# Four more block products in quarter blocks, variances summed on ScalarE, one buffer for two products, in a four-layer graph kernel

## The chip, the cores and the metric

One core of a Trainium2 chip runs the whole kernel. Its engines are TensorE (PE, with PEld for its weight loads), VectorE (DVE), ScalarE (ACT), GpSimd (POOL) and SyncE (SP, which here only issues DMAs). Each engine executes its own instructions in the order in which they were put into its queue, and waits where an operand or a buffer isn't ready. The metric is the device time of one execution in microseconds, the median of several runs.

## The reference

128 graphs share one adjacency matrix of 128 nodes; each node has 512 features, all in float32. Four layers follow each other, each with a residual and a layernorm over the features.

```python
# x (128,128,512), adj (128,128)
def _L0(x):                       # GCN
    norm_adj = adj * rsqrt(deg)[:, None] * rsqrt(deg)[None, :]
    return einsum('nm,bmo->bno', norm_adj, einsum('bni,io->bno', x, weight)) + bias
def _L1(x):                       # W1 = W2 = adj
    A, C = adj @ x, adj @ x + b
    return max(relu(A[:, :, None, :] + (C - A)[:, :, :, None]), axis=-1)
def _L2(x):
    q, k, v = x @ Wq.T, x @ Wk.T, x @ Wv.T
    rel = adj.T[None] * einsum('bnd,bmd->bnm', q, k)
    rel = rel / norm(rel, axis=2, keepdims=True)
    return einsum('bnm,bmd->bnd', rel, v)
def _L3(x):                       # mask = adj, ALPHA = 0.2
    h = x @ W
    s1, s2 = h @ a[:512], h @ a[512:]
    e = leaky_relu(s1[:, :, None] + s2[:, None, :], ALPHA) * mask
    att = softmax(e, axis=2)
    return elu(att @ h + beta * h)
x = layernorm(x + L0(x)); x = layernorm(x + L1(x)); x = layernorm(x + L2(x)); x = layernorm(x + L3(x))
```

## The kernel before, in words

**Groups.** The 128 graphs are 32 groups of four (GB = 4). A group's `x` is one tile of 128 nodes x 4 graphs x 512 features that stays in SBUF from its load to its store. Layer 1 adds to a row a number that is the same for all its features (C - A is b), and the layernorm behind it takes that out again. So layers 0 and 1 together need one large product, layer 2 two, layer 3 one:

- `w`: `y` (x aggregated with the normalised adjacency, computed by the steps `y00` to `y11`) times the layer-0 weight. Its result is added to `x`; the two layernorms behind it are one, with other constants (`var`, case "w").
- `z`: the transposed `x` (`xT`) with the product of Wq and Wk (`gq`), laid down in C of z; `r` (line 905) multiplies it with `xT` to give q times k.
- `v`: `xT` with Wv, laid down in C of v; `f` (line 953) multiplies it with the normalised `rel`, and `fa` (line 963) adds it to `x`.
- `k`: `nT`, the transposed `x` after layer 2, with the layer-3 weight, laid down in C of k; `h` (line 953) multiplies it with the attention, and `em`, `ee`, `ea` form elu and the sum into `x`.

**Block products.** Each of the four products is done as seven products P1 to P7 of half size in place of eight (Strassen's scheme in Winograd's form), in the order 1, 2, 5, 7, 6, 3, 4. One block product is four matmuls of 128x256 (`make`, line 565). The left operands' sums are made by POOL (`sum`: steps `sy`, `sx`; tile `S`), the results are joined by ACT copies (`c`, `t`), DVE additions (`d`) and a POOL addition (`u`). The number behind a step's letter is the block product: `z6` is P6 of z, and P6, P3 and P4 add onto the banks of P1, P5 and P7.

**Quarter blocks.** A block product can itself be done by the same scheme on 128x128 blocks: seven matmuls of 128x128 (`make_small`, line 529; four first and three then, the three called with a second digit: `k28` is the second part of P2 of k). Before the three, ACT copies part of the bank away (`before`, steps `b..`, tile `q`) and DVE joins (`between`, steps `e..`, three operations, line 378). The left operand needs four sums of 128x128 on POOL (`small`, line 426, steps `ly`, `lx`, `ln`), the weight three sums more (`w_small`, made once). Before the change this is so for P2 of w, P1 and P2 of z and v, and P2 of k: six per group. The names are in `SMALL`; the sums of `xT` for P1 and P2 are kept in the tile `L`, because z and v both use them; those of P2 of y and n overwrite a part of the tile itself that isn't read any more (`room`).

**Turning.** `xT` and `nT` are made by DVE transposes of 32x32 squares (`xt`, `nt`, line 459) and 16 DMAs on SP's queue that exchange the squares (`xd`, `nd`, line 465). `rel` and the attention are turned likewise through DRAM (`wr`, `cr`, `aw`, `cat`). In the last group TensorE transposes `rel` and the attention.

**Layernorm.** `st` (bn_stats and bn_aggr on DVE, line 770), `va`, `po` (POOL), `nb`, then `ap` (ACT, line 796).

**Order.** Nothing is scheduled by a program at run time: three strings of steps, HEAD, TURN and TAIL, list every step as `group.step`, and each engine gets its instructions in that order. TURN is repeated with the group numbers raised by one: 21 turns, for groups 5 to 25 before the change. In one turn the work of four groups is interleaved: w of one group, z and v of the one before, k two before that, and the layernorm and store of a fourth. A tile of a pool is a slot that is used again by later groups; who writes to it first waits until the last reader of its earlier content is done. The pool `big` gives three slots to a name unless `bufs` says otherwise.

The lines that hold the order around P5 of z, before the change (group numbers relative):

```python
2.ea3 3.ex3 2.stk0 6.sy3 3.k7 3.ck5 2.stk1 6.bi01 2.stk2 3.k2 3.dk7 3.k6 3.bk2 2.stk3 3.ek2 3.k3
3.tk 3.uk11 2.vak 3.rd 3.k28 3.dk3 2.pok 3.k4 3.dk2 5.lx1 4.f0 2.nbk 4.f1 4.fa0 5.sx0 2.apk0
4.f2 3.dk4 2.apk1 2.fin0 5.lx2 4.fa1 4.f3 2.apk2 2.fin1 4.fa2 2.apk3
```

Of the kernel before, what the change touches and what calls it, by code (L numbers as in the profile page):

```python
# [41 lines left out]
EPS = 1e-5  # L43
# [3 lines left out]
GB = 4  # L47
# [3 lines left out]
FIRST = 5  # L51
LAST = -6
# [15 lines left out]
0.sq2 1.nbw s.mv1 0.sq3 1.apw0 0.v2 2.sy3 0.cv5 1.xt0 0.cr 1.apw1 0.v7 0.dv2 0.rp 1.apw2 1.xt1
2.bi10 1.apw3 1.xt2 0.v6 0.dv7 2.bi00 1.xt3 0.v3 0.tv 1.xd s.mv2 0.uv11 0.v4 0.dv3 2.bi11 0.f0
0.dv4 2.bi01 0.f1 0.fa0 0.f2 0.stv0 0.f3 0.fa1 0.fa2 3.y10 0.fa3 3.y00 3.cy10 3.bi10 0.stv1  # L70
3.y11 3.cy00 0.stv2 3.bi00 3.y01 3.cy11 0.stv3 3.sy0 2.w1 3.cy01 0.vav 0.pov 2.w5 2.dw1 3.sy1
2.w7 0.nbv 2.dw5 1.lx1 0.apv0 0.apv1 0.nt0 2.w2 0.apv2 2.dw7 1.sx0 0.nt1 2.w6 0.apv3 0.nt2 1.lx2
2.bw2 2.ew2 2.w3 2.tw 0.nt3 1.sx1 0.sc00 2.w28 1.sx2 2.dw3 2.w4 0.sc01 3.ly2 0.sc10 1.z1 0.nd
0.sc11 1.z5 1.bz1 1.sx3 0.sc20 1.ez1 3.sy2 1.z2 0.sc21 1.z18 1.bz2 2.uw01 0.sc30 1.z7 1.cz1
1.ez2 1.cz5 3.sy3 1.z6 0.sc31 2.uw10 1.dz7 2.dw2 2.uw11 1.z28 2.dw4 1.z3 3.bi11 1.dz2 1.tz
2.stw0 1.z4 1.uz11 0.pw 1.dz3 2.stw1 3.bi01 1.r0 1.dz4 2.stw2 1.r1 0.sn0 2.stw3 1.r2 0.pe 0.sn1
2.vaw 1.r3 1.v1 1.rm 2.pow 1.sq0 1.v5 0.sn2 1.bv1 0.pl0 1.ev1 0.pl1 0.sn3 0.pl2 1.v2 0.pl3 1.sq1
1.rt 1.v18 0.ej 1.bv2 1.v7 1.wr 1.cv1 1.ev2 1.sq2 1.cv5 2.nbw 0.ei 1.v6 2.apw0 1.dv7 2.apw1
2.xt0 1.cr 2.apw2 1.v28 2.xt1 1.v3 1.tv 1.dv2 2.apw3 1.uv11 2.xt2 0.ex0 2.xt3 1.v4 0.ex1 1.dv3
0.ex2 0.ex3 3.w1 2.xd 1.dv4 1.sq3 0.rd 1.rp 3.w5 3.dw1 0.so0 0.so1 3.w7 3.dw5 0.at 3.w2 3.dw7  # L80
3.w6 3.bw2 3.ew2 3.w3 3.tw 3.uw01 3.w28 3.uw10 3.dw3 0.aw 3.w4 3.dw2 3.uw11 3.stw0 1.f0 3.dw4
1.f1 3.stw1 2.lx1 0.cat 1.f2 3.stw2 1.f3 3.stw3 2.sx0 0.k1 1.fa0 2.lx2 3.vaw 1.fa1 0.k5 1.fa2
0.ck1 1.fa3 2.sx1 1.stv0 0.k7 0.ck5 2.sx2 1.stv1 1.stv2 3.pow 0.k2 0.dk7 2.sx3 0.k6 0.dk2 3.nbw
1.stv3 3.apw0 0.k3 s.m32 0.tk 3.apw1 3.xt0 0.uk11 3.apw2 0.k4 0.dk3 3.apw3 3.xt1 3.xt2 4.y10
0.dk4 4.y00 4.cy10 4.bi10 3.xt3 4.y11 4.cy00 1.vav 3.xd 4.bi00 4.y01 4.cy11 4.sy0 0.h0 4.cy01
0.h1 0.em0 4.sy1 0.h2 0.ee0 0.em1 0.ea0 4.sy2 0.h3 0.ee1 0.em2 2.z1 4.ly2 0.em3 0.ee2 2.z5 0.ea1
2.bz1 0.ee3 2.ez1 4.sy3 2.z2 0.ea2 1.pov 2.z18 2.bz2 0.ea3 2.z7 2.cz1 2.ez2 4.bi11 2.cz5 0.stk0
4.bi01 2.z6 2.dz7 0.stk1 2.z28 2.tz 3.sx0 0.stk2 2.z3 2.dz2 2.uz11 0.stk3 2.z4 2.dz3 3.sx1 0.vak
2.r0 1.nbv 2.dz4 0.pok 1.apv0 2.r1 1.apv1 1.nt0 3.sx2 2.r2 1.apv2 0.nbk 2.r3 1.apv3 1.nt1 3.sx3
1.nt2 0.apk0 2.v1 2.rm 0.apk1 0.fin0 2.v5 1.nt3 2.bv1 0.fin1 0.apk2 2.ev1 2.v2 0.apk3 0.fin2  # L90
2.rt 2.sq0 2.v18 0.fin3 1.sc00 2.bv2 2.v7 2.wr 2.cv1 2.ev2 2.sq1 2.cv5 1.sc01 2.v6 2.sq2 2.sq3
5.ld 2.dv7 2.rp 2.cr 1.sc10 2.v28 2.tv 1.sc11 2.v3 3.lx1 2.dv2 1.sc20 2.v4 2.uv11 2.dv3 1.sc21
3.lx2 3.z1 1.sc30 1.nd 2.dv4 3.z5 3.bz1 3.ez1 3.z2 1.sc31 3.z18 3.bz2 3.ez2 3.z7 3.cz1 3.cz5
3.z6 3.dz7 3.z28 3.tz 3.z3 3.dz2 3.uz11 3.z4 1.pw 3.dz3 3.r0 3.dz4 3.r1 1.sn0 3.r2 1.pe 1.sn1
3.r3 2.f0 3.rm 1.sn2 2.f1 3.sq0 2.fa0 3.sq1 1.ln2 2.f2 2.stv0 1.pl0 1.pl1 2.f3 2.fa1 1.pl2 1.pl3
1.sn3 2.fa2 4.w1 3.sq2 3.sq3 2.fa3 1.ej 2.stv1 4.w5 4.dw1 3.rp 2.stv2 4.w7 4.dw5 2.stv3 4.w2
4.dw7 2.vav 4.w6 4.bw2 1.ei 2.pov 4.ew2 1.ex0 1.ex1 4.w3 3.rt 1.ex2 1.ex3 2.nbv 3.wr 2.apv0 1.rd
4.w28 4.dw3 1.so0 2.apv1 4.w4 2.nt0 2.apv2 1.so1 4.dw2 2.apv3 2.nt1 3.v1 3.cr 2.nt2 4.tw 3.v5
3.bv1 2.nt3 4.uw01 3.ev1 4.uw10 2.nd 3.v2 1.at 3.v18 3.bv2 4.uw11 4.stw0 3.v7 3.cv1 3.ev2 3.cv5
4.dw4 3.v6 3.dv7 4.stw1 3.v28 3.tv 4.stw2 3.v3 3.uv11 4.stw3 3.dv2 3.v4 3.dv3 4.vaw 2.sc00 4.pow  # L100
5.y10 3.dv4 1.aw 5.y00 5.cy10 5.bi10 5.y11 5.cy00 4.nbw 2.sc01 5.bi00 4.apw0 5.y01 2.sc10 4.apw1
1.k1 2.sn0 1.cat 4.xt0 4.apw2 2.sc11 4.apw3 2.sn1 1.k5 4.xt1 1.ck1 4.xt2 5.cy11 2.sn2 4.xt3
5.cy01 1.k7 1.ck5 2.ln2 2.sc20 2.sc21 1.k2 1.dk7 2.sn3 1.k6 1.bk2 2.sc30 1.ek2 5.sy0 1.k3 1.tk
2.sc31 5.sy1 2.pw 1.k28 1.dk3 1.uk11 1.k4 1.dk2 5.ly2 3.f0 4.xd 1.dk4 5.sy2 3.f1 3.fa0 3.f2
3.stv0 5.bi11 3.f3 3.fa1 3.fa2 5.sy3 1.h0 3.fa3 1.h1 5.bi01 1.em0 1.h2 1.em1 1.ee0 1.h3 1.em2
1.ee1 2.k1 1.ea0 1.ee2 1.em3 1.ea1 1.ee3 2.k5 1.ea2 2.ck1 1.ea3 2.pe 2.k7 1.stk0 2.ck5 1.stk1
1.stk2 2.k2 2.dk7 4.lx1 2.k6 2.bk2 2.pl0 2.ek2 2.pl1 2.pl2 2.k3 2.pl3 4.sx0 1.stk3 2.tk 3.stv1
4.lx2 2.k28 1.vak 3.stv2 2.k4 3.stv3 4.sx1 2.dk3 4.z1 3.vav 4.sx2 2.dk2 4.z5 4.bz1 2.dk4 1.pok
4.ez1 4.z2 4.sx3 4.z18 4.bz2 1.nbk 4.ez2 2.ej 4.z7 1.apk0 4.cz1 1.fin0 3.pov 2.ei 1.apk1 4.z6
1.apk2 2.uk11 1.fin1 1.apk3 1.fin2 4.z28 3.nbv 4.cz5 1.fin3 4.dz2 4.tz 4.z3 4.dz7 2.ex0 2.ex1  # L110
4.uz11 2.ex2 4.z4 4.dz3 2.ex3 6.ld 3.apv0 2.rd 2.so0 4.r0 4.dz4 3.apv1 3.nt0 4.r1 3.apv2 2.so1
3.nt1 3.apv3 4.r2 3.nt2 4.r3 3.nt3 5.w1 2.at 3.nd 4.rm 3.sc00 4.sq0 5.w5 4.sq1 5.dw1 4.sq2
3.sc01 4.sq3 5.w7 4.rp 5.dw5 3.sc10 3.sc11 5.w2 5.dw7 5.w6 5.bw2 3.sc20 5.ew2 5.w3 5.tw 3.sc21
5.uw01 3.sc30 5.w28 5.uw10 5.dw3 2.aw 5.w4 5.dw2 5.uw11 3.sc31 4.v1 5.dw4 3.pw 4.v5 4.bv1 5.stw0
3.sn0 2.cat 4.ev1 3.sn1 4.v2 5.stw1 4.v18 4.bv2 3.sn2 5.stw2 3.pe 4.v7 4.cv1 4.ev2 3.ln2 4.cv5
# [12 lines left out]
2.aw 3.vav 3.pov 4.z4 4.dz3 3.nbv 3.apv0 2.cat 4.r0 4.dz4 3.apv1 3.nt0 4.r1 3.apv2 3.sc00 3.apv3
# [1031 lines left out]
```

## Time and profile before

| | us |
|---|---|
| median of 3 runs (lowest, highest) | 2022.32 (2022.27, 2022.95) |
| the profiled execution | 2021.49 |
| its span | 2019.7 |
| PE busy, share of the span | 1992.9, 99% |
| DVE busy | 1645.2, 81% |
| POOL busy | 1330.2, 66% |
| ACT busy | 829.7, 41% |
| one turn | 61.38 |

The span lasts from the first to the last instruction of the profiled execution; its time has 1.8 us more around it. Busy time is the sum over an engine's instructions, so overlaps with other engines aren't seen in it. The profile's matmul rows count each float32 matmul as two (it makes two passes). In a row such as `x<-p_w,x` the tile written stands left of the arrow, those read right of it, with buffer numbers left out. A release `<-DVE e L972` names the engine and the line whose result ended a wait.

Three of the costliest groups of instructions, from the list of the page (columns: line, engine, operation, tiles, shape, count, busy us, mean ns of one, idle time before them and its releaser):

```profile
L796 ACT ACTIVATE x<-x,nb,r 128x512 f32<-128x512 f32 x383 | 282.5, 804 | 188.9 <-DVE nb L790 176.9
L381 POOL TENSOR_TENSOR x<-x,bias_bc 128x512 f32<-128x512 f32 x128 | 162.7, 1291 | 37.1 <-PE py L736 28.9
L770 DVE BATCH_NORM_STATS2 st_v<-x 128x6 f32<-128x512 f32 x128 | 87.2, 681 | 0.2
```

### The profile page before, as it was taken

Reading aid. Unit: us, or ns where it says so; the run is one execution under the profiler, and the core shown is the slowest. Engines: PE = TensorE matmul, PEld = TensorE weight load, DVE = VectorE, ACT = ScalarE, POOL = GpSimd, SP = SyncE. Lnnn points to the kernel's source line nnn. Section 1 sums busy time; section 2 is a strip of 40 time slices with the busy share of each in tenths; the row PEclk is TensorE's granted clock in tenths of the full one; section 3 lists DMA queues with packets and bytes.
Section 4 is the critical chain, followed back from the end, with each engine's and each line's share of the span. In section 5 each row is a group of like instructions: output and inputs, shape, how many; then the busy total and the mean of one; then the engine's idle time right before and its main releaser. Section 6 shows DMA issues by size and latency. Waiting matters only on the chain.

```text
span 2019.7 us, 32758 instructions
## 1 busy us (share of the span) xinstructions
PE 1992.9 (99%) x10921; PEld 1715.3 (85%) x10921; DVE 1645.2 (81%) x3490; ACT 829.7 (41%) x1797; POOL 1330.2 (66%) x1429
## 2 busy tenths in 40 slices
PE   9899999999999999999999999999999999999997
PEld 8798888888888888888888888888888888888875
DVE  6878788888888888888888888888888888888886
ACT  2234334444344443444443444433444434444344
POOL 7677557766668666677666677666676668567551
PEclk9999999999999999999999999999999999999998
DMA  7433344443444444434344444444344444443443
GB/s 225 82 66 80 68 87 103 90 78 90 102 90 96 83 83 97 95 91 97 69 95 105 89 94 83 81 94 103 89 97 75 87 101 88 96 102 65 70 85 88
DMA packets 737975, 184.78 MB, mean 91 GB/s; under 512 B 689936, under 2 KB 690320, under 8 KB 737808
## 3 DMA queue, kind: packets, MB, share of 16 engines
q1 hardware_dynamic: 737664, 182.56, 41.8%
q8 instruction: 88, 1.44, 0.3%
q14 instruction: 79, 0.65, 0.1%
q10 hardware_dynamic: 144, 0.13, 0.0%
HBM read 64.55 MB, written 49.87 MB: 57 GB/s over the span
## 4 chain that ended last, share of the span: by engine, by line
PE 97%; SPq 1%; DVE 1%; DMA 0%; issue 0%; ACT 0%; POOL 0%; DVEq 0%; POOLq 0%
PE p_k L565 16%; PE p_w L565 16%; PE p_z L565 14%; PE p_v L565 13%; PE pr L905 6%; PE py L736 6%; PE pl_v L953 5%; PE pl_k L953 5%; PE p_z L529 5%; PE p_v L529 5%; PE p_k L529 2%; PE p_w L529 2%; SPq L465 1%; PE pk L827 1%; DVE e L972 0%
## 5 line engine op out<-in xcount | busy, mean ns | idle before, releaser
L796 ACT ACTIVATE x<-x,nb,r 128x512 f32<-128x512 f32 x383 | 282.5, 804 | 188.9 <-DVE nb L790 176.9
L381 POOL TENSOR_TENSOR x<-x,t_w 128x512 f32<-128x512 f32 x96 | 120.8, 1285 | 122.1 <-ACT t_w L375 122.1
L381 POOL TENSOR_TENSOR x<-x,bias_bc 128x512 f32<-128x512 f32 x128 | 162.7, 1291 | 37.1 <-PE py L736 28.9
L378 DVE TENSOR_TENSOR x<-p_w,x 128x512 f32<-128x512 f32 x192 | 129.4, 687 | 57.6 <-PE p_w L565 38.6
L972 DVE SCALAR_TENSOR_TENSOR e<-x,wa_bc 128x512 f32<-128x512 f32 x256 | 173.2, 676 | 3.8 <-ACT x L796 0.9
L384 POOL TENSOR_TENSOR r<-n,minus_half 128x4 f32<-128x4 f32 x32 | 32.4, 1012 | 174.5 <-ACT pr L920 174.5
L384 POOL TENSOR_TENSOR r<-v,minus_half 128x4 f32<-128x4 f32 (+1 forms) x99 | 98.9, 999 | 52.8 <-DVE v L782 44.4
L736 PEld LDWEIGHTS py<-nadjT,x 128*128 128x128 f32 x1024 | 120.3, 193 | 2.8 <-DVE nadjT L633 0.8
L963 DVE SCALAR_TENSOR_TENSOR x<-pl_v,r,x 128x512 f32<-128x512 f32 x128 | 90.1, 743 | 39.5 <-PE pl_v L953 38.7
L565 PE MATMUL p_z<-S_x,gq 128*128 128x256 f32 x512 | 121.2, 380 | 0.0
L565 PE MATMUL p_v<-wvT,S_x 128*128 128x256 f32 x512 | 121.1, 379 | 0.0
L565 PE MATMUL p_z<-S_x,gq_t 128*128 128x256 f32 x512 | 121.1, 379 | 0.0
L736 PE MATMUL py<-nadjT,x 128*128 128x128 f32 x1024 | 120.6, 277 | 0.4 <-DVE nadjT L633 0.4
L565 PE MATMUL p_v<-wvT_t,S_x 128*128 128x256 f32 x512 | 121.0, 379 | 0.0
L565 PE MATMUL p_w<-w_t,S_y 128*128 128x256 f32 x512 | 121.0, 379 | 0.0
L565 PE MATMUL p_w<-w,S_y 128*128 128x256 f32 x512 | 120.9, 379 | 0.0
L565 PE MATMUL p_k<-w_t,S_n 128*128 128x256 f32 x496 | 118.4, 382 | 0.0
L565 PE MATMUL p_k<-w,S_n 128*128 128x256 f32 x496 | 117.2, 379 | 0.0
L953 PE MATMUL pl_v<-C_v,relT 128*128 128x512 f32 x248 | 111.6, 592 | 0.0
L953 PE MATMUL pl_k<-C_k,attT 128*128 128x512 f32 x248 | 111.5, 592 | 0.0
L1061 DVE SCALAR_TENSOR_TENSOR x<-pl_k,x 128x512 f32<-128x512 f32 x127 | 86.8, 688 | 29.7 <-PE pl_k L953 29.4
L565 PEld LDWEIGHTS p_w<-w,S_y 128*128 128x128 f32 x512 | 97.3, 190 | 13.2
(1580 smaller groups left out, 5425.2 us busy)
## 6 DMA issues: line engine op xcount, KB each, us to landing
out_dram<-x SPq DMA_DIRECT2D x127, 256.0 KB, 2.0
x<-in_x_dram SPq DMA_DIRECT2D x31, 1024.0 KB, 5.3
d_r<-ru SPq DMA_DIRECT2D x31, 256.0 KB, 2.3
relT<-d_r SPq DMA_DIRECT2D x124, 64.0 KB, 2.5
s<-d_s SPq DMA_DIRECT2D x31, 256.0 KB, 3.7
d_a<-au SPq DMA_DIRECT2D x31, 256.0 KB, 2.0
attT<-d_a SPq DMA_DIRECT2D x124, 64.0 KB, 2.5
x<-in_x_dram SPq DMA_DIRECT2D x2, 512.0 KB, 4.4
```

The lines of the kernel that those rows point to most:

```text
L378: nc.vector.tensor_tensor(o, a, b, f)
L381: nc.gpsimd.tensor_tensor(o, a, b, f)
L384: nc.gpsimd.tensor_tensor(o, v, minus_half[:, : v.shape[-1]], ALU.pow)
L529: nc.tensor.matmul(self.banks[i][:, r, bass.ts(c, P)], lhsT=lhsT, rhs=rhs, start=(not then and n == 0), stop=(n == len(steps) - 1), skip_g ...
L565: nc.tensor.matmul(ps[:, j, :], lhsT=lhsT, rhs=rhs, start=(i not in ONTO and j == 0 and kc == 0), stop=(j == 1 and kc == 1), skip_group_ch ...
L736: nc.tensor.matmul(o, lhsT=self.x_chunk(b, kc), rhs=nadjT, start=True, stop=True)
L796: nc.scalar.activation(xt, xt, AF.Identity, bias=self.nb[k][:, b : b + 1], scale=self.rstd[k][:, b : b + 1],)
L905: nc.tensor.matmul(self.pr[:, b, :], lhsT=self.whole["z"][:, fc, b // 2, bass.ts(b % 2, P)], rhs=self.xT.chunk(b, fc), start=(fc == 0), st ...
L953: nc.tensor.matmul(ps, lhsT=left[:, b, :], rhs=self.whole[k][:, b, :], start=True, stop=True)
L963: nc.vector.scalar_tensor_tensor(xt, self.pf[b], self.rnorm[:, b : b + 1], xt, ALU.mult, ALU.add)
L972: nc.vector.scalar_tensor_tensor(wide(self.e), self.x[:, b, :], 1.0, wide(wa_bc[k]), ALU.mult, ALU.mult, accum_out=self.s[:, k, b : b + 1],)
L1061: nc.vector.scalar_tensor_tensor(xt, self.pz[b], 0.0, xt, ALU.max, ALU.add)
```

## The change

- **Quarter blocks.** P1 of w, P5 of z and v, and P1 of k are done by quarter blocks too: ten per group in place of six. POOL makes 12 more sums of 128x128 per group (`ly1`, `ln1`, `lx5`). Those for P1 of y and of n go into a new tile `l` with one slot, shared by the two; `L` has room for three sets. The second part of a small product is split into two steps (`18` and `19`: the first of the three matmuls, and the other two).
- **Variances of the layernorms of layers 2 and 3.** `fa` and `ea` write the rows' sums as they add (`accum_out`), DVE scales them (`mn`), ACT squares the centred `x` with the sum of squares as a by-product (`vq`, eight per turn; the squares themselves go into relT or attT and aren't read), and `var` and `shift` take these sums. bn_stats and bn_aggr fall away there, except for the last group.
- **Buffers.** C of z and C of v share one slot; rel and relT share a name; Setup's tiles move to other slots.
- **Attention.** The scaling by 1/den (`so0` to `so3`) is done by ACT, one graph at a time, in place of one POOL operation.
- **Ends.** x of group 0 and n of the last group are transposed by TensorE and copied by ACT (`xp`, `xc`, `np`, `nc`) in place of the exchange; s2 of the last group comes from four matmuls of 128x512.
- **Weight sums** for quarter blocks are made by POOL.
- **Order.** HEAD, TURN and TAIL are written anew; TURN runs for groups 6 to 26 (21 turns).

The part of the new TURN around P1 of k and the end of a turn, with the steps that end the turn:

```python
2.h2 2.ee0 2.em1 6.bi00 2.h3 2.em2 2.ee1 3.k1 6.ly2 2.em3 2.ee2 3.k7 2.ea0 3.bk1 2.ee3 3.ek1
6.ly1 3.k5 2.ea1 2.ea2 6.sy2 3.k18 3.k19 2.ea3 3.k2 3.ck1 6.bi11 2.mnk0 3.pw 2.mnk1 2.mnk2
2.vqk0 2.mnk3 3.k6 6.sy3 3.ck5 3.bk2 3.dk7 3.k3 2.vqk1 6.bi01 3.ek2 2.vqk2 5.lx1 3.pe 3.k28
3.k29 2.vqk3 3.k4 3.dk2 3.tk 2.vak 5.sx0 3.dk3 4.f0 3.dk4 5.sx1 3.pl0 4.f1 4.fa0 3.pl1 3.pl2
5.lx5 4.f2 4.fa1 3.pl3 4.f3 4.fa2
```

The first steps of TURN, which follow there with all numbers one lower for the same group (`4.z1` is z of the group that was 5):

```python
4.z1 3.mnv0 4.lx2 3.fa3 3.vqv0 4.z5 3.mnv1 3.mnv2 4.bz1 3.mnv3 3.vqv1 4.z7 4.ez1 4.sx2 3.vqv2
```

And around P1 of w:

```python
3.nt1 6.ld 5.w5 2.ex0 5.dw7 2.ex1 3.nt2 2.ex2 3.nt3 5.w1 2.ex3 5.dw5 3.nd 5.w4 5.bw1 2.rd 2.so0
5.ew1 2.so1 2.so2 2.so3 5.w18 5.dw4 2.so4 5.w19 5.w2 5.dw1 2.at 5.w3 5.bw2 5.ew2 5.w6 5.dw3
```

The diff without the three strings, cut to what the text speaks of:

```diff
-    def w_small(w, m, i):
-        b = lambda k, j: w[:, 2 * (i - 1) + k, bass.ts(j, P)]
+    def w_small(w, t, m, i):
+        of = w_blocks(w, t)[i]
+        b = lambda k, j: of[:, k, bass.ts(j, P)]
         return dict(
...
     W = {k: w_blocks(*v) for k, v in weights.items()}
-    SMALL = ("02", "g1", "g2", "v1", "v2", "32")
+    SMALL = ("01", "02", "g1", "g2", "g5", "v1", "v2", "v5", "31", "32")
     w_m = {k: wts.tile([P, 3, P], F32, name=f"m_{k}") for k in SMALL}
-    W2 = {k: w_small(weights[k[0]][0], m, int(k[1])) for k, m in w_m.items()}
+    W2 = {k: w_small(*weights[k[0]], m, int(k[1])) for k, m in w_m.items()}
...
         def small(self, i):
-            a = lambda b, k: self.chunk(b, 2 * (i - 1) + k)
+            of = self.s[:, 0] if i == 5 else self.block(0, i - 1)
+            a = lambda b, k: of[:, k, b, :]
             s = self.room(i)
...
         def room(self, i):
-            return [self.chunk(2 + n // 2, n % 2) for n in range(4)]
+            if i == 2:
+                return [self.chunk(2 + n // 2, n % 2) for n in range(4)]
+            t = big.tile([P, 4, P], F32, tag="l", name=f"l_{self.name}", bufs=1)
+            return [t[:, n] for n in range(4)]
...
+        def turn(self, b, x):
+            ps = bank(f"pt_{self.name}_{b}")
+            for kc in range(KC):
+                nc.tensor.transpose(ps[:, kc, :], x[:, bass.ts(kc, P)], ident)
+            self.banks[b] = ps
+        def take(self, b, sums):
+            if b == 0:
+                self.aT = big.tile([P, KC, GB, P], F32, tag="aT", name=f"{self.name}T")
+                if sums:
+                    self.s = big.tile([P, 4, 2, 2, P], F32, tag="S", name=f"S_{self.name}")
+            copy(self.aT[:, :, b, :], self.banks[b])
         def move(self):
...
             if i == 1:
-                self.l = big.tile([P, 2, 4, P], F32, tag="L", name=f"L_{self.name}", bufs=1)
-            return [self.l[:, i - 1, n] for n in range(4)]
+                self.l = big.tile([P, 3, 4, P], F32, tag="L", name=f"L_{self.name}", bufs=1)
+            return [self.l[:, {1: 0, 2: 1, 5: 2}[i], n] for n in range(4)]
...
-        def make_small(self, i, then=False):
-            if not then:
+        def make_small(self, i, then):
+            if then is None:
                 self.banks[i] = psum.tile([P, 2, HD], F32, tag="bank", name=f"p{i}_{self.name}")
             A, B = self.left.smalls[i], W2[f"{self.weight}{i}"]
-            steps = self.THEN_SMALL if then else self.FIRST_SMALL
+            steps = {None: self.FIRST_SMALL, 8: self.THEN_SMALL[:1], 9: self.THEN_SMALL[1:]}[then]
             for n, (r, c, a, b) in enumerate(steps):
...
             if i in self.left.smalls:
-                self.make_small(i, then is not None)
+                self.make_small(i, then)
                 return
...
         def xd(self):
-            self.xT.move()
+            if self.g:
+                self.xT.move()
+        def xp(self, b):
+            self.xT.turn(b, self.x[:, b, :])
+        def xc(self, b):
+            self.xT.take(b, True)
...
         def nd(self):
-            self.nT.move()
+            if not self.end:
+                self.nT.move()
+        def np(self, b):
+            self.nT.turn(b, self.x[:, b, :])
+        def nc(self, b):
+            self.nT.take(b, False)
...
+        def mean(self, k, b):
+            of = self.nm[k][:, b : b + 1]
+            nc.vector.tensor_scalar(of, of, -1.0 / D, None, ALU.mult)
+        def square_sum(self, k, b, junk):
+            if b == 0:
+                self.ss[k] = self.small("ss")
+            nc.scalar.activation(
+                wide(junk),
+                self.x[:, b, :],
+                AF.Square,
+                bias=self.nm[k][:, b : b + 1],
+                accum_out=self.ss[k][:, b : b + 1],
+            )
+        def row_sums(self, k, b):
+            if self.end:
+                return {}
+            if b == 0:
+                self.nm[k] = self.small("nm")
+            return dict(accum_out=self.nm[k][:, b : b + 1])
         def var(self, k, b=None):
...
             b = slice(0, GB) if b is None else slice(b, b + 1)
+            if k in self.ss:
+                nc.vector.tensor_scalar(self.var_[k], self.ss[k], 1.0 / D, EPS, ALU.mult, ALU.add)
+                return
             v, var = self.var_[k][:, b], self.mv[k][:, b, 1]
...
             b = slice(0, GB) if b is None else slice(b, b + 1)
+            if k in self.ss:
+                tt(self.nb[k], self.nm[k], self.rstd[k], ALU.mult)
+                return
             nc.vector.scalar_tensor_tensor(
...
                 shape = [P, KC, 2, 2 * P] if k == "z" else [P, GB, D]
-                self.whole[k] = big.tile(shape, F32, tag=f"{k}C", name=f"C_{k}_{self.g}", bufs=1)
+                tag = "kC" if k == "k" else "C"
+                self.whole[k] = big.tile(shape, F32, tag=tag, name=f"C_{k}_{self.g}", bufs=1)
                 self.po[k].block = lambda p, h: self.c_block(k, p, h)
...
         def rm(self):
-            self.rel = mid.tile([P, GB, P], F32, tag="rel", name=f"rel_{self.g}")
+            self.rel = mid.tile([P, GB, P], F32, tag="relT", name=f"rel_{self.g}")
             tt(self.rel, self.pr, adjT_b, ALU.mult)
...
             nc.vector.scalar_tensor_tensor(
-                xt, self.pf[b], self.rnorm[:, b : b + 1], xt, ALU.mult, ALU.add
+                xt, self.pf[b], self.rnorm[:, b : b + 1], xt, ALU.mult, ALU.add, **self.row_sums("v", b)
             )
...
             if self.end:
-                s2 = lambda b: self.s[:, 1, b : b + 1].to_broadcast([P, P])
-                self.s2 = self.transpose("ps2", s2).rearrange("p b j -> p j b")
+                ps = bank("ps2")
+                for kc in range(KC):
+                    wa2 = setup.wa_[:, 1, kc : kc + 1].to_broadcast([P, P])
+                    nc.tensor.matmul(
+                        wide(ps),
+                        lhsT=wa2,
+                        rhs=wide(self.nT.aT[:, kc]),
+                        start=(kc == 0),
+                        stop=(kc == KC - 1),
+                    )
+                self.s2 = ps.rearrange("p b j -> p j b")
                 return
...
                 nc.vector.scalar_tensor_tensor(e, e, rden, beta_i, ALU.mult, ALU.add)
-            elif i == 0:
-                pool_tt(self.e, self.e, self.rden.unsqueeze(2).to_broadcast([P, GB, P]), ALU.mult)
+            elif i < GB:
+                e = self.e[:, i, :]
+                nc.scalar.activation(e, e, AF.Identity, scale=self.rden[:, i : i + 1])
             else:
...
             xt = self.x[:, b, :]
-            nc.vector.scalar_tensor_tensor(xt, self.pz[b], 1.0, xt, ALU.min, ALU.add)
+            nc.vector.scalar_tensor_tensor(
+                xt, self.pz[b], 1.0, xt, ALU.min, ALU.add, **self.row_sums("k", b)
+            )
```

## The prediction

> **What bounds the kernel now.** I read the page's busy shares first, then the chain that ended last, then the windows of single turns and of the two places with holes, then TensorE's waits.
>
> ```profile
> PE 1992.9 (99%) x10921; PEld 1715.3 (85%) x10921; DVE 1645.2 (81%) x3490; ACT 829.7 (41%) x1797; POOL 1330.2 (66%) x1429
> ...
> PE 97%; SPq 1%; DVE 1%; DMA 0%; issue 0%; ACT 0%; POOL 0%; DVEq 0%; POOLq 0%
> ```
>
> ```profile
> 54.60:62.71 8.11, 0.02 (x1) 0.03 (x1) 7.99 (x16) 0.59 (x1) 2.87 (x3) 0.79 0.65 92
> 952.12:1013.50 61.38, 61.38 (x341) 53.01 (x340) 50.77 (x108) 25.99 (x56) 41.62 (x46) 1.00 0.43 91
> 1013.50:1074.88 61.38, 61.38 (x341) 53.01 (x340) 50.09 (x108) 25.83 (x56) 41.59 (x46) 1.00 0.43 91
> 1966.66:1970.54 3.88, 0.00 (x0) 0.03 (x1) 3.81 (x9) 1.12 (x2) 0.50 (x1) 1.00 0.66 100
> 1970.00:1975.10 5.10, 1.51 (x5) 0.77 (x5) 4.89 (x15) 0.00 (x0) 0.00 (x0) 0.57 0.67 102
> 1975.10:1978.60 3.50, 3.50 (x10) 2.75 (x10) 3.40 (x9) 1.14 (x4) 1.27 (x1) 0.50 0.46 114
> ```
>
> ```profile
> PE p_z L565 <- DMA x_0T<-sq_x: 8.1, 1, 8.1
> PE ps L896 <- DVE e L972: 6.9, 4, 3.9
> ```
>
> The columns of the windows are PE, PEld, DVE, ACT and POOL busy, then the granted clock. A turn is 61.38 us of matmuls in 61.38 us: nothing waits in the middle, so a matmul saved there is time saved, as long as nothing else becomes late. TensorE's holes are at the two ends.
>
> **1. Quarter blocks.** A whole block product starts 1.73 us after the one before it (1004.22, 1005.95, 1007.67); a quarter-block product takes 0.89 us (1003.33 to 1004.22) plus 0.67 (1007.67 to 1008.34), 1.56 in all:
>
> ```profile
> 1003.33 0.38 PE L529 MATMUL p_k<-w,n_14T 128*128 128x128 f32 x2
> 1003.55 0.61 PE L529 MATMUL p_k<-m,n_14T 128*128 128x128 f32 x4
> 1004.00 0.39 PE L529 MATMUL p_k<-w,n_14T 128*128 128x128 f32 x2
> 1004.22 1.89 PE L565 MATMUL p_k<-w_t,S_n 128*128 128x256 f32 x8
> 1005.95 1.89 PE L565 MATMUL p_k<-w,S_n 128*128 128x256 f32 x8
> 1007.67 0.61 PE L529 MATMUL p_k<-w,n_14T 128*128 128x128 f32 x4
> ```
>
> The built program has 492 fewer 128x256 and 861 more 128x128 matmuls: 123 products (z5, v5, w1 31 each, k1 30). 123 x 0.165 = **-20.3 us**; a full turn falls to 61.38 - 4 x 0.165 = 60.72.
>
> **2. Other engines, per turn.** ACT gains eight Squares of 128x512. The trace has none; the 128x512 Identity (0.80) and the 128x128 Square plus its accumulator read (0.28 + 0.19) bound one at 0.71 to 0.99, so 8 x 0.85 = 6.8. With four copies of 0.37 and four scalings of about 0.35, ACT goes from 26 to 36. DVE loses 8 x (0.68 + 0.18) of statistics and gains 4 x 1.23 of joining, 8 accumulator reads of 0.08 and 8 one-column scalings of 0.15: 50.4 - 6.9 + 6.8 = 50.3. POOL gains 12 sums of 0.45 and loses one 1.04: 46. All lie below 60.7, so by load TensorE still binds; the shared buffer C costs nothing, since the last reader of C of v (f) is issued before z's first copy and the last of z (r) before v's. The 32 exchange issues fewer on SP only bring loads forward. The square's unused result goes to relT or attT, read for the last time by f or h just before, and rel takes a slot of relT: 0, by the same order. The ten weight sets' sums go to POOL (40 x 0.45 = 18 us; DVE had 24 such sums); TensorE has other groups' products there: 0, at most +2.
>
> **3. Start.** x_0's exchange becomes 16 transposes (four take 0.43, so 1.72). The hole of 8.09 goes, and with it the slow clock after it: z of group 0 took 14.00 us, where seven block products at full clock take 12.09. Group 0's products run earlier, before other groups' x can fill (x_0 lands at 12.0): a new 1.55 of idle. -8.09 - 1.91 + 1.72 + 1.55 = -6.7. Group 1 and 3 then run nearer to their sums and joins (z5, pr): some 0.2 to 0.7 each, +1.7 (0 to 3). **-5.0**.
>
> **4. The small buffer "l", the step that decides.** Quarter sums of y and of n share one buffer. In the built program POOL's first sum for ly1 of group g+2 waits for the first matmul of k19 of g-1, the last reader of n's sums; it is written ahead of k5 in the order, so without that wait POOL could take it 2 us earlier or more (k5 1.73 and k18 0.22). Behind it on POOL stand, in order, sy2, bi11, sy3, bi01, lx1, sx0, sx1 and lx5 of g+1, and z5's second matmul of that next group needs lx5's third sum. The durations:
>
> ```profile
> 1057.35 2.50 POOL L381 TENSOR_TENSOR S_y<-y_18T 128x512 f32<-128x512 f32 x2
> 1059.81 1.28 POOL L381 TENSOR_TENSOR S_y<-S_y,y_18T 128x512 f32<-128x512 f32 x1
> 1061.04 1.83 POOL L381 TENSOR_TENSOR y_18T<-y_18T 128x128 f32<-128x128 f32 x4
> 1062.83 1.28 POOL L381 TENSOR_TENSOR S_y<-y_18T,S_y 128x512 f32<-128x512 f32 x1
> ```
>
> Pitch 1.23 for 128x512, 1.79 for four of 128x128. POOL: 1.79 + 4 x 1.23 + 1.79 + 2 x 1.23 + 1.29 = 12.25, plus some 0.3 to hand over (a matmul's end 0.165, then 0.08 as from py at 1053.58 to bias at 1053.66, and again). TensorE's work from k19 to that matmul: 0.22 + k2 0.89 + k6, k3 3.45 + k28, k29 0.67 + k4 1.73 + f 3.43 + z1 0.89 + 0.22 = 11.50. Late by 1.05; 0.75 if the handovers cost nothing, 1.45 at the sums' mean durations of 1.29. It comes once for each of groups 6 to 27: 22 x 1.0 = **+22** (16 to 32). A second small wait: between w1's first four matmuls and w19 TensorE has w4 and one matmul, 1.95; the end 0.165, ACT's copy 0.37, the three joins 1.23 and three handovers of 0.08 make 2.0 to 2.15. About 0.15 x 29 groups = **+4** (0 to 6).
>
> VectorE's small operations can stand still beside a POOL sum:
>
> ```profile
> 497.46 1.20 DVE L790 SCALAR_TENSOR_TENSOR nb<-mv_w,r 128x4 f32<-128x4 f32 x1
> ```
>
> ```profile
> 497.36 1.27 POOL L381 TENSOR_TENSOR C_v<-C_v,t_v 128x512 f32<-128x512 f32 x1
> ```
>
> This nb ended with the POOL sum; at 472.01, with POOL free, the same took 0.16. The change adds eight one-column scalings per turn, small operations too, which the trace of before doesn't have. The four of k stand just ahead of dk7 and the joins of k2, where POOL begins ly1; held like nb, by sums of 0.45, they take 4 x 0.45 = 1.8 in place of 0.6, held by 128x512 sums 4.9. Behind them wait dk7 (0.69) and the joins (1.23), which k29 needs 3.7 us after k2's first part (k6, k3, k28): 2.5 to 6.8 us of work, so at worst 3 us late, of which 1 falls into the wait for lx5. I take 0 (0 to +2 per turn): the row's nearest case is sums of 0.45, and then all fits.
>
> The Trainium skill, "SBUF — State Buffer", section "SBUF: two separate sides", speaks against the change: it says that VectorE, in a two-port mode or with two SBUF inputs, and GpSimd lock each other out for a whole instruction. By it, an estimate is that every scaling beside POOL costs POOL its own time as well, 8 x 0.15 in a turn, of which half lies in the chain to lx5: 13 us more in all. The trace doesn't bear that out: POOL's C_v sum beside nb took 1.27 as elsewhere.
>
> **5. End.** s2 of the last group becomes four 128x512 matmuls, 3.43 for four transposes (0.43), and n_31's transposes add 1.72: +4.7. The holes at ps (6.92) and the slow clock after (blocks of 3.48 and 2.92 for 1.73: 2.94) go: -9.9. New: s2, pl 1.14, e by adj 1.27, maximum 0.65, exponentials 1.55, division and four small products 1.4, with em, ee and ea of group 30 between (about 1.9), against h of group 30 (3.43): a hole of 3.1 to 4.5 before pat. The row above shows a half clock after a hole of 3.9, so 1.8 (0 to 3) more, an estimate below its 2.94 because the transposes of e after the hole are short. In the last groups the late ly1 pushes e by adj of group 26 back behind ly1 and three sums (5.5 us after k19), then maximum, four exponentials 1.6, a copy, a Square, two Identities and w1's copy on ACT: joins end 13.9 to 15.5 after k19 while TensorE has 13.3 of work: 1.0 to 2.5. The same lateness, DVE and ACT behind TensorE, stands in the built program's order at z of 29 (twice), k28 of 28, and k5 and k2 of 30: 1 each, an estimate (0 to 2), five times. 4.7 - 9.9 + 3.8 + 1.8 + 1.7 + 5 = **+7** (0 to 13).
>
> Sum: -20.3 - 5.0 + 22 + 4 + 7 = +7.7 on the profiled execution's 2021.49 (span 2019.7): 2029.2. The median of the runs stands 0.83 above that execution: **2030 us**. All low ends of 3, 4 and 5 together give 2011, all high ends 2049; as they seldom meet, 2020 to 2040 is this case's own range.
>
> **Rivals.**
> - *TensorE alone binds* (20%): ly1 is not late enough to reach z5. For it: POOL is only 66% busy now. It needs POOL's chain under 11.2 us, which at 1.23 a sum it is not. Steps 1, 3 and a third of 5: 2022.3 - 20.3 - 5 + 2 + 2 = 2001, faster.
> - *POOL stall alone* (17%): the end gains what its old holes lose (5 at 0 or below), w19 fits: 2022.3 - 20.3 - 5 + 22 + 0 = 2019 (2015 to 2027). For it: single waits at the end are the least certain rows.
> - *VectorE held by POOL* (8%): the scalings' 8 meetings per turn, 8 x 1.0, make DVE 57 of 61 and show at k29 with 0.7 beyond the wait for lx5 in 22 turns: 2030 + 15 = 2045. Slower by more than the forecast. For it: nb's 1.2 us. Against it: the lx5 wait covers the same time. It decides from where DVE's joins of k2 end over 4.7 us after k2's first part.
> - *As forecast* (55%): 2020 to 2040.
>
> **How the numbers follow.** Differences within 0.2% (4 us) can't be told from no change: faster is below 2018.3, slower above 2026.4. The forecast gives slower 0.46, same 0.08, faster 0.01; the POOL stall alone same 0.10, slower 0.03, faster 0.04; TensorE alone faster 0.17, same 0.03; VectorE held slower 0.08. Together faster 0.22, same 0.21, slower 0.57. The range 2011 to 2041 leaves out most of the first rival (0.14) and part of the third (0.06).
>
> **What would show it.** Right: turns of 61.6 to 62.1 us, TensorE waiting about 1 us once a turn at p_z's second small product for POOL's L_x, POOL idle ahead of l_y until k19; no hole at 54 us; a hole of 3 to 4.5 us before pat. Wrong: turns of 60.7 (the first rival), waits at p_k's second part for DVE (the third), POOL sums at another pitch.

## The result

The changed kernel takes 2047.95 us (median of 4 runs, 2045.56 to 2048.86) where the one before takes 2022.3 (2021.91 to 2022.95): a ratio of 1.0125, 95% interval 1.0107 to 1.0142, so about 26 us slower. The profiled execution's span grew by 23.8 us, from 2019.7 to 2043.5. The forecast had the direction, but not the size: +7.7 us, and 2041 as the top of its range. The kernel before was timed again beside each run below; its medians there are 2022.3 to 2023.3.

The page of the kernel after, its busy shares and the chain that ended last:

```profile
PE 1995.7 (98%) x11695; PEld 1724.3 (84%) x11695; DVE 1623.9 (79%) x3820; ACT 1096.5 (54%) x2548; POOL 1471.1 (72%) x1806
...
PE 74%; POOL 14%; DVE 4%; issue 3%; DMA 2%; SPq 1%; ACT 1%; POOLq 0%; DVEq 0%; ACTq 0%
```

TensorE's share of the chain fell from 97% to 74%, and POOL holds 14% of it: part of the time is now set by POOL's sums. A busy share can't show that, for TensorE is still at 98% and POOL at only 72%. Nor is 14% the loss: in a turn the chain runs over POOL for some 12 us (see below), 13% of the span in 22 turns, while TensorE loses 1.0 us there.

Turns, in the windows view (PE, PEld, DVE, ACT, POOL busy, granted clock):

```profile
953.78:1016.00 62.22, 61.34 (x366) 53.25 (x364) 50.53 (x120) 33.99 (x81) 45.63 (x57) 1.00 0.43 90
1016.00:1078.22 62.22, 61.34 (x365) 53.25 (x364) 50.78 (x120) 34.47 (x81) 45.62 (x57) 1.00 0.43 90
1078.22:1140.45 62.23, 61.34 (x366) 53.25 (x364) 50.66 (x120) 34.40 (x81) 45.64 (x57) 1.00 0.42 90
```

A turn takes 62.22 us in place of 61.38, though its matmuls need only 60.72 by their pitches (a pitch is the time from one matmul's start to the next one's: 0.223, 0.432 and 0.858 for 128, 256 and 512 columns). The difference of 1.50 is waiting; PE's idle time shows 0.88 of it, since a row lasts until its matmul's end, some 0.16 after the next could have begun.

The same count over the whole run, each stretch's time less the pitches of its matmuls, between the first rows of f (`pl_v`) of the groups:

| waits, us | before | after | change | forecast |
|---|---|---|---|---|
| to f of group 0 | 16.4 | 12.0 | -4.5 | -8.5 |
| f of 0 to f of 5 | 0.3 | 3.9 | +3.6 | +2.4 |
| f of 5 to f of 27 (22 groups) | 0.2 | 33.1 | +32.9 | +25.3 |
| f of 27 to the end | 21.3 | 26.9 | +5.7 | +2.6 |
| matmul work | 1981.5 | 1967.6 | -13.9 | -13.9 |

(The forecast's column spreads its steps over these stretches. The sum of changes is 23.8, the span's. Pitches are those at full clock, so time lost to a lower clock counts as waiting here.)

Where the turn waits, in TensorE's timeline. First P5 of z:

```profile
957.88 0.39 PE L578 MATMUL p_z<-L_x,gq 128*128 128x128 f32 x2
958.11 0.39 PE L578 MATMUL p_z<-S_x,gq_t 128*128 128x128 f32 x2
959.23 0.71 PE L578 MATMUL p_z<-L_x,m_g 128*128 128x128 f32 x4 [0.74 <-POOL L_x L412]
959.78 0.39 PE L578 MATMUL p_z<-L_x,gq_t 128*128 128x128 f32 x2
```

The first of P5's matmuls starts at 958.11; the second should follow at 958.33 and starts at 959.23, when POOL's L_x comes. With 0.10 more inside the next row this is 1.00 us. The view counts 0.74 of it as idle, 16.2 us in 22 waits. On POOL, one turn later:

```profile
1004.12 1.82 POOL L412 TENSOR_TENSOR y_17T<-y_17T 128x128 f32<-128x128 f32 x4
1009.16 0.87 POOL L412 TENSOR_TENSOR l_y<-y_17T 128x128 f32<-128x128 f32 x2 [3.22 <-PE p_k L578]
1009.99 0.46 POOL L412 TENSOR_TENSOR l_y<-l_y,y_17T 128x128 f32<-128x128 f32 x1
...
1020.95 0.46 POOL L412 TENSOR_TENSOR L_x<-L_x,S_x 128x128 f32<-128x128 f32 x1
```

POOL stands still for 3.22 us with eight more steps queued, until TensorE's p_k (k19, the last reader of l_n) is done; lx5's third sum then ends at 1021.41, 12.25 us after l_y began. The second place in the turn is P1 of w:

```profile
973.93 0.39 PE L578 MATMUL p_w<-w,l_y 128*128 128x128 f32 x2
974.16 1.89 PE L614 MATMUL p_w<-w_t,y_16T 128*128 128x256 f32 x8
976.19 0.46 PE L578 MATMUL p_w<-w,y_16T 128*128 128x128 f32 x2
976.49 0.39 PE L578 MATMUL p_w<-w,l_y 128*128 128x128 f32 x2
```

```profile
974.41 0.37 ACT L406 COPY q_w<-p_w 128x256 f32<-128x256 f32 x1 [1.05 <-PE p_w L578]
974.82 0.29 DVE L409 TENSOR_TENSOR q_w<-p_w,q_w 128x128 f32<-128x128 f32 x1 [0.52 <-ACT q_w L406]
975.14 0.90 DVE L409 TENSOR_TENSOR p_w<-p_w,q_w 128x128 f32<-128x128 f32 x2
```

The copy and the three joins of P1 of w end at 976.04. w4 starts at 974.16 and should be followed at 975.89; w18 starts at 976.19, and w19 0.30 after it in place of 0.22: 0.38 in all. Only 0.14 of it is idle time by the rows, since w4's last row is drawn to 976.05, and the timeline puts no bracket there. A remaining 0.12 lies at P6 of k.

### The profile page after: what moved, and what is told of

It reads as the page before. It is cut to its first block, busy times and chain, and to the rows that moved or that the text cites. A ratio compares the mean times of both kernels' runs of the same rounds, so it can differ in the third digit from the quotient of the medians.

```text
span 2043.5 us, 36294 instructions
## 1 busy us (share of the span) xinstructions
PE 1995.7 (98%) x11695; PEld 1724.3 (84%) x11695; DVE 1623.9 (79%) x3820; ACT 1096.5 (54%) x2548; POOL 1471.1 (72%) x1806
## 4 chain that ended last, share of the span: by engine, by line
PE 74%; POOL 14%; DVE 4%; issue 3%; DMA 2%; SPq 1%; ACT 1%; POOLq 0%; DVEq 0%; ACTq 0%
PE p_v L614 10%; PE p_w L614 10%; PE p_z L614 10%; PE p_v L578 7%; PE p_k L614 7%; PE p_z L578 6%; PE pr L1002 5%; PE pl_k L1050 5%; PE py L786 5%; PE p_w L578 5%; POOL L_x L412 4%; POOL S_x L412 3%; POOL S_y L412 3%; PE p_k L578 2%; POOL l_y L412 2%
## 5 line engine op out<-in xcount | busy, mean ns | idle before, releaser
L412 POOL TENSOR_TENSOR e<-e,beta_i 128x512 f32<-128x512 f32 x31 | 39.5, 1273 | 139.8 <-ACT e L1138 139.8
L846 ACT ACTIVATE relT<-x,nm 128x512 f32<-128x512 f32 x124 | 89.6, 722 | 71.8 <-PE pl_v L1050 63.3
L409 DVE TENSOR_TENSOR C_k<-p_k,C_k 128x512 f32<-128x512 f32 x62 | 42.7, 689 | 88.8 <-ACT C_k L406 54.0
L406 ACT COPY q_v<-p_v 128x256 f32<-128x256 f32 x93 | 34.2, 368 | 146.2 <-PE p_v L578 135.7
L614 PEld LDWEIGHTS p_w<-w_t,S_y 128*128 128x128 f32 x512 | 97.3, 190 | 13.2
```

The lines of the kernel that those rows point to most:

```text
L409: nc.vector.tensor_tensor(o, a, b, f)
L412: nc.gpsimd.tensor_tensor(o, a, b, f)
L614: nc.tensor.matmul(ps[:, j, :], lhsT=lhsT, rhs=rhs, start=(i not in ONTO and j == 0 and kc == 0), stop=(j == 1 and kc == 1), skip_group_ch ...
L846: nc.scalar.activation(wide(junk), self.x[:, b, :], AF.Square, bias=self.nm[k][:, b : b + 1], accum_out=self.ss[k][:, b : b + 1],)
```

## The experiments

**Theory A**: the slot shared by ly1 and ln1 holds POOL's whole queue behind k19 (1.0 us at z5 in every turn), and the joins of P1 of w aren't covered by w4 (0.38). **Theory B**: the added squares, row sums and scalings make ScalarE and VectorE late. **Theory C**: POOL's 12 additional sums are too long in themselves.

**e1: ly1 behind lx5.**

```diff
 (TURN)
-... 3.ek1 6.ly1 3.k5 2.ea1 2.ea2 6.sy2 ... 5.lx5 4.f2 ...
+... 3.ek1 3.k5 2.ea1 2.ea2 6.sy2 ... 5.lx5 6.ly1 4.f2 ...
```

> In each of the 21 turns the sums ly1 are put behind lx5 on POOL's queue instead of ahead of sy2; nothing else changes. Theory A (the buffer that ly1 and ln1 share holds POOL's whole queue behind k19): the wait of about 1.0 us at z5's second small matmul goes, the one at the second part of P1 of w (0.38) and that at P6 of k (0.12) stay; a turn falls from 62.22 to about 61.2, the span by 21 x 1.0 to about 2022. Theory B (ScalarE and VectorE are late through the added squares and row scalings, and POOL only shows it): a turn stays at 62.0 to 62.3 and the wait moves to another releaser. Theory C (POOL's 12 sums more make its stretch from y to lx5 too long in itself): the wait shrinks by no more than half, turn 61.7 or more.

Measured 2028.06 us, ratio to the kernel before 1.0029 (1.0018 to 1.0040), span 2026.1; a turn takes 61.21. One turn, and TensorE's longest waits in the run (total, times, longest):

```profile
824.67:885.88 61.21, 61.07 (x365) 53.18 (x364) 48.48 (x119) 34.63 (x82) 45.64 (x57) 1.00 0.43 91
```

```profile
PE pat L993 <- DVE e L1135: 2.8, 1, 2.8
PE p_k L578 <- DVE x L1175: 2.6, 1, 2.6
PE p_w L578 <- DVE p_w L409: 2.5, 2, 2.3
```

The wait for L_x, 16.2 us in 22 places, is no longer at the head; it is 0.9 in two places, at 111 and 401 us, ahead of the first moved step. The squares are still there, so B doesn't make this wait. POOL does the same sums in the same turn, 45.64 us busy as before; but ly1's own 1.79 us have also left the stretch ahead of lx5, more than the 1.0 that was lost, so e1 alone doesn't part A from C. POOL's rows above do: it stood idle for 3.22 us ahead of l_y, and without that lx5's third sum would, by these rows, have ended some 2.2 us before TensorE needed it. So C falls. The step is worth 1.01 us per turn. The span is 4 us above the 2022 expected; the difference lies outside the turns.

**e3: the second part of P1 of w after the first of P2.**

```diff
 (TURN)
-5.ew1 2.so1 2.so2 2.so3 5.w18 5.dw4 2.so4 5.w19 5.w2 5.dw1
+5.ew1 2.so1 2.so2 2.so3 5.dw4 2.so4 5.w2 5.w18 5.w19 5.dw1
```

> In each turn the last three small matmuls of P1 of w (w18, w19) are issued after the first part of P2 (w2) instead of around it. Theory A (the joins of P1 of w take 2.1 us from its first part, and w4 alone, 1.73, covers them, since the wait stands ahead of w18): the 0.38 goes, turn 61.84, span lower by 21 x 0.38 = 8 to about 2035; z5's wait stays at about 1.0. Theory B (VectorE is late there): the wait stays or moves to w2's joins, turn 62.1 or more.

2042.2 us, ratio 1.0094 (1.0081 to 1.0108), turn 61.84:

```profile
826.57:888.41 61.84, 61.10 (x365) 53.33 (x364) 50.26 (x120) 34.20 (x81) 45.62 (x57) 1.00 0.43 90
```

The 0.38 goes, to the hundredth, and z5's wait stays. VectorE's joins are no earlier; TensorE has 0.89 us more to do before it needs them.

**e4: both.**

> Both reorderings together. Theory A: turn 60.72 plus 0.1 to 0.2 at k, 60.85; span 2043.5 - 21 x 1.37 = about 2015, below the kernel before. Theory B: turn above 61.5, span above 2030. Theory C: turn 61.3 or more.

2020.86 us, ratio 0.9988 (0.9980 to 0.9997); turn 60.84. The windows view of one:

```profile
762.83:823.67 60.84, 60.84 (x365) 53.26 (x364) 50.21 (x121) 34.53 (x82) 46.54 (x59) 1.00 0.43 92
```

TensorE is busy all of it again, and 60.84 is its 60.72 of matmuls plus the 0.12 at k. Two moved steps undo the loss of the turns. The span of the profiled execution (2022.7) is 8 us above what was expected, but that execution is the slowest of eleven; their spans run from 2014.8 to 2022.7, with 2018.8 in the middle. By the count of waits its excess lies outside the turns: 15.1 to the first f (a wait of 2.8 us for the first weight, and P1 of w of group 1 waited 2.5), 12.2 from f of 26 to f of 31. Part of both is the clock: at five of its holes of 2.0 to 2.8 us TensorE was granted half its clock for 3.4 us, and lost some 1.6 each time. Two of the five lie ahead of the first f. In the changed kernel's profile, whose hole before pat is as long, this came once between the first and the last 10 us. One of the five, with the granted clock third from the end:

```profile
69.96:73.37 3.41, 3.41 (x15) 3.21 (x15) 1.77 (x4) 0.37 (x1) 1.90 (x2) 0.50 0.67 243
```

**e6: P1 of w and of k as whole products.**

```diff
-    SMALL = ("01", "02", "g1", "g2", "g5", "v1", "v2", "v5", "31", "32")
+    SMALL = ("02", "g1", "g2", "g5", "v1", "v2", "v5", "32")
 (HEAD, TURN, TAIL)
-  g.ly1 g.w18 g.w19 g.bw1 g.ew1 g.ln1 g.k18 g.k19 g.bk1 g.ek1 s.m01 s.m31
```

> P1 of w and P1 of k are whole block products again (their steps ly1, ln1, b, e, 18 and 19 are taken out of the order); P5 of z and v by quarter blocks, squares on ScalarE, shared buffer C and the new ends stay. Theory A: no shared small buffer, no early second part of w1: a turn is TensorE's work alone, 60.72 + 2 x 0.165 = 61.05 to 61.15; with 61 whole products (10 us of matmuls more) and 22 x 1.5 of waits less the span is about 2020. Theory B: the squares are still there, so waits of 1 us or more per turn stay, turn 62 or more.

2015.89 us, ratio 0.9966 (0.9954 to 0.9978), turn 61.05: TensorE's work and nothing else.

```profile
817.03:878.08 61.05, 61.05 (x353) 53.10 (x352) 45.04 (x113) 33.88 (x79) 42.29 (x49) 1.00 0.43 91
```

With 10 us more of matmuls it beats both the changed kernel and the one before. It is 6.5 below the expected span, because the waits outside the turns go too: 9.0 to the first f, 1.0 on to the sixth, 5.9 over the last groups.

**e5: statistics back on VectorE**, in e4.

```diff
 (row_sums)
-            if self.end:
+            if True:
                 return {}
...
-                self.mean(kind[2:], *n)
+                self.stats(kind[2:], *n)
...
-                self.square_sum(kind[2:], *n, junk=self.relT if kind[2:] == "v" else self.attT)
+                pass
```

> From the kernel with both reorderings (e4, turn 60.84): the layernorms of layers 2 and 3 go back to bn_stats and bn_aggr on VectorE, at the places where the row scalings stood; the squares on ScalarE and the row sums fall away. Theory B (the added squares, row sums and scalings make the waits): a turn falls to the matmuls' own 60.72 and the few waits of 0.1 go, span at or below 2022. Theory A (they cost nothing, and VectorE needs the relief): VectorE does 8 x (0.86 - 0.15 - 0.08) = 5 us more per turn, four of the eight directly ahead of the joins of z's P1, so a wait appears there for VectorE: turn 61.3 to 62.4, span 2035 to 2060.

2082.14 us, ratio 1.0288 (1.0271 to 1.0305), turn 62.96: a wait of up to 1.5 us at z's P1 for VectorE's joins, where A has it, and 2.2 of waiting per turn in all. It is more than A expected (62.4 and 2060 at the most), so A had the place and the engine but too small a size. B falls for good: without the squares on ScalarE this order is 61 us slower than e4. This is the worth of the part at its places in the new order, not that of bn_stats where the old order had it. What TensorE waits for there:

```profile
PE p_z L578 <- DVE p_z L409: 37.1, 27, 1.5
```

**e7 and e8: the quarter blocks of P1 of w and k in the turns alone.** From e4: in most of HEAD and TAIL these products are whole again; ly1 of group 7 goes behind lx5 in HEAD, and a few products of s of the last group behind ee and ea of group 30.

> From e4: in HEAD (groups 1 to 6) and TAIL (groups 29 to 31) P1 of w, and in HEAD (1, 2) and TAIL (27 to 30) P1 of k, are whole products again (13 fewer quarter-block products, 2.1 us of matmuls more); ly1 of group 7 goes behind lx5 as in the turns; two to three products of s of the last group go behind ee and ea of group 30. Theory A (what e4 still loses is the same late joins and late ly1 in HEAD and TAIL, which e6 didn't have: waits of 15.1 to the first f, 3.7 on to the sixth and 12.2 over the last groups against 9.0, 1.0 and 5.9): turn stays 60.84, span about 2022.7 + 2.1 - 6 - 2.7 - 5 = 2010, the fastest of all. Rival (those waits hang on when the first loads land and on the exchange's DMAs, which differ from run to run): span 2018 or more, waits to the first f above 11.

2005.91 us (ratio 0.9919, 0.9904 to 0.9934), span 2006.0, turn 60.84; waits of 9.9 to the first f, 1.2 on to the sixth, 5.7 from f of 26 to f of 31. The trace has 15 quarter-block products fewer than e4's, not 13. The rival (landing times that differ from run to run) isn't what makes e4 slower, since the four executions of e7 (2005.5 to 2008.0) all lie below the eleven of e4 (2016.9 to 2024.8). Nor did the first weight land late in e4's profile: at 12.0 there, at 12.8 here. But the 15.1 isn't P1 of w alone either, since 3.3 of it was lost at half clock, and e7's trace has no such stretch ahead of its first f. What e7 computes isn't the four layers: its whole products of P1 use a weight block that already holds a difference in one quarter. e8 mends that. Its edit against e7 (the steps s.m01 and s.m31, which make the differences, come later, and s.n01 and s.n31, which take them back, are new):

```diff
 (HEAD)  ... 2.k4 s.m31 ...  6.w3 s.m01 ...
 (TAIL)  ... 5.dw1 s.n01 ...  3.ek2 s.n31 ...
+            elif kind == "n":
+                b = W2[f"{n[0]}{n[1]}"]
+                tt(b["t3"], b["b22"], b["t3"], ALU.subtract)
...
-            for i in (1, 2):
+            for i in (2,):
                 b = W2[f"3{i}"]
                 tt(b["t3"], b["b22"], b["t3"], ALU.subtract)
```

> As e7, with the weights' in-place differences for P1 of w and of k made only after the last whole P1 of HEAD and taken back before the first whole P1 of TAIL: in e7 those whole products used a weight block of which one quarter already held a difference. Two operations of 128x128 on VectorE more, eight sums on POOL later: the time is that of e7, span 2004 to 2010, turn 60.84, waits to the first f below 11.

2006.97 us, ratio to the kernel before 0.9919 (0.9905 to 0.9932): 16 us faster than before and 41 faster than the change as it was made. The waits to the first f are 9.5, a turn takes 60.84. From its page the busy shares and the chain that ended last, then its longest waits:

```profile
PE 1983.2 (99%) x11605; PEld 1723.7 (86%) x11605; DVE 1570.8 (78%) x3776; ACT 1085.3 (54%) x2533; POOL 1444.7 (72%) x1746
...
PE 95%; DVE 2%; DMA 1%; SPq 1%; POOL 1%; issue 0%; ACT 0%; DVEq 0%; POOLq 0%; ACTq 0%
```

```profile
PE pat L991 <- DVE e L1133: 2.8, 1, 2.8
PE pl_v L1048 <- DMA relT<-d_r: 2.5, 1, 2.5
PE p_w L609 <- DMA w<-in_L_gnn_weight_dram: 1.4, 1, 1.4
```

Apart from the 0.12 at k in each turn, what is left are single waits at the two ends. POOL is busy for as large a share as in the changed kernel (72%), but holds 1% of the chain in place of 14%.

Not tried: two slots for the small buffer, which would take 2 KB per partition more. So the shared slot is shown by POOL's idle row and by moving the step that waits for it, not by a second slot.

## Why the prediction was right in direction and wrong in size

The forecast's sum was short by 16 us of the profiled execution's 23.8: 4 at the start, 1 up to f of group 5, 8 in the turns, 3 at the end. Another 1.6 lies between that execution and the median, which is 2.4 above it, while the forecast added 0.8 as before. A turn is 62.22, just outside the 61.6 to 62.1 that were to show the forecast right. No one term is off by the whole; the largest part is the cover of P1 of w's joins, 0.23 more in every turn.

- **Step 1, matmuls: right.** In e4 a turn is 60.84, the forecast 60.72 plus 0.12; the work falls by 13.9 us over the run, -20.3 and +6.4 at the ends, as summed.
- **Step 2, loads: right.** ACT 34.4 per turn (forecast 36), DVE 50.7 (50.3), POOL 45.6 (46); a Square of 128x512 takes 0.72 and its accumulator read 0.19, inside the bounds of 0.71 to 0.99. The shared buffer C, priced at nothing, costs nothing in a turn: e6 has it, and its turn is TensorE's work alone.
- **Step 4, the shared slot: right, to a few hundredths.** The chain on POOL measured 12.25 (forecast 12.25), z5's wait 1.00 (1.05, taken as 1.0), in 22 groups. That both meet to a few hundredths is partly luck, as the step itself allowed 0.75 to 1.45.
- **Step 4, P1 of w: the step that failed.** The prediction let "w4 and one matmul, 1.95" cover the joins. The wait stands ahead of w18, not behind it, so only w4's 1.73 covers them: 0.38 in place of 0.15, 22 x 0.23 = 5 us. The step took it that after the split into 18 and 19 only w19 waits; by the rows it is w18. e3 shows it: with w2 ahead of w18 the 0.38 is gone. The same product outside the turns brought single waits that the sum didn't list, such as group 1's:

```profile
67.99 0.46 PE L578 MATMUL p_w<-w,y_1T 128*128 128x128 f32 x2 [1.90 <-DVE p_w L409]
```

- **A wait left out:** P6 of k adds onto P1's bank and waits 0.12 per turn, 2.6 us in 22 turns, for which the sum has no term. By the order it waits for ACT's copy of C_k, which ends 0.14 ahead of it; it goes in e6, where P1 of k is whole, but no run changes the copy alone. Since e4 still has it, it is no part of the shared slot's 1.0.
- **Step 3, start: too good by 4 us.** The 8.09 hole and the slow clock behind it went, as forecast; but P1 of w of group 1 waited 1.90, and three small waits of z of group 0 (for x_0T, S_x and C_z) cost 1.5 by the pitches. The new idle time of 1.55 came as 1.86. It ends when the first weight lands, at 12.70; the "x_0 lands at 12.0" of the step is that weight in the trace of before, where x_0 has landed by 6.5. In the other runs but e5 this wait is 0.9 to 2.8. In e7, where P1 of w of group 1 is whole, waits to the first f are 9.9 in place of 12.0.
- **Step 5, end: too good by 3 us.** The hole before pat is 2.8 by the view (forecast 3.1 to 4.5), and w of 29 waited 1.3 (1.0 to 2.5). The half clock didn't come behind that hole, where it was priced at 1.8: the granted clock is 1.00 from 2016.9 to 2020.3. It came at the wait of P2 of k of group 30, 0.50 from 1995.4 to 1998.8, and cost 1.5. The five late places, priced at 1 each, came as 2.6 (P2 of k of 30), 1.3 (P2 of k of 28), 0.6 (P5 of k of 30) and hardly anything at z of 29. What the sum didn't list are 1.5 at f of 30 (for the exchange of relT), 0.8 at ps (for the copies of n_31T) and 1.1 more behind the last matmul. Why the last is longer no run here shows.
- **The range**: each wait near zero was given about its own size upward, and the bounds of 3, 4 and 5 were then narrowed because they "seldom meet". They met: the misses of the four stretches have one sign. All high ends together, 2049, would have held the result.
- **Rivals.** TensorE alone: what the turns of e4 and e6 show once the steps are moved. POOL stall alone: the stall came, but w1's joins weren't covered and the end's waits grew by 5.7. VectorE held by POOL: it didn't happen. The one-column scalings took 0.15 each even beside POOL's sums (the one at 1019.45 ran within a sum of S_x, from 1017.65 on, the three from 1020.31 within sums of L_x); the operations of 128x4 were held, nb for 0.95 on average and v (from the sums of squares) for 0.43, and no wait of TensorE in the turns leads to them. Nor did the scalings hold POOL up, which the prediction priced at 13 us: its sums with a scaling inside them took 1.27 at 128x512 (36 of them) and 0.46 at 128x128 (29), as those without. The row of nb that the prediction set against that price couldn't show it, as POOL's sum had begun 0.10 before nb.

## What to carry to other kernels

When two producers share a slot, look at what stands behind the waiting one on its in-order queue: here sums that nobody needed for 25 us held back eight steps, and TensorE stood waiting for the last of them. In this kernel a place further back in the queue cured it, for no memory. And when you count what covers a wait, put it on the instruction that carries it in the built program: on an engine without slack, 0.38 us per turn were 8 us of the run.

## What the runs showed that was not expected

- The same sums at the same load (POOL 45.6 us per turn) cost 1.0 us per turn or nothing, by their order alone.
- nb of 128x4 is held by a POOL sum (948 ns on average over 62; 0.15 to 0.16 us in the eight that met none), a scaling of 128x1 isn't (146 ns on average over 248, never above 154, with 107 of them wholly inside a POOL instruction):

```profile
L409 DVE TENSOR_TENSOR nb<-nm,r 128x4 f32<-128x4 f32 x62 | 58.8, 948 | 47.1 <-POOL r L415 47.1
L840 DVE TENSOR_SCALAR nm<-nm 128x1 f32<-128x1 f32 x248 | 24.1, 146 | 0.0
```

- Of each wait of TensorE the first 0.16 us or so don't show as idle time: e4's turn is busy for 60.84 of 60.84 us and still has the 0.12 at k, and of w18's 0.30 only 0.14 is idle. The pitches show them.
